# First cross attention of a Perceiver stack: score tiles of 32 by 32, two units a step in one PSUM tile, probabilities transposed on VectorE, one division a batch

## The chip, the cores and the metric

The kernel runs on one core of a Trainium2 chip. The metric is device time in microseconds (us), from one launch that holds the whole network. Three runs of the kernel before gave 3168.56, 3169.97 and 3195.57 us; the median is 3169.97 us.

## The reference, cut to what matters

The network has four layers of cross attention, self mixing (attention or a state space block) and feed-forward. Only the first block of the first layer is touched. It reads 16 batches of 64 query tokens with 256 channels and, per batch, 1024 context tokens with 192 channels.

```python
def _L0_xattn_ref(q_tokens, kv_tokens, Wq, Wk, Wv, Wo):   # (16,64,256), (16,1024,192)
    q = q_tokens @ Wq.T; k = kv_tokens @ Wk.T; v = kv_tokens @ Wv.T
    # 16 heads of 16 channels: (16, 16, 64 or 1024, 16)
    attn = einsum('bhqd,bhkd->bhqk', q, k) / sqrt(16)
    attn = softmax(attn, axis=-1)
    out = einsum('bhqk,bhkd->bhqd', attn, v)
    return merge_heads(out) @ Wo.T
x = x + _L0_xattn_ref(layernorm(x), ctx_768, Wq, Wk, Wv, Wo)
```

Everything is float32. A matmul of float32 stands in the trace as two records of load and two of multiply, so 4 matmuls appear as x8.

## The kernel before

The function is `xattn_direct`. Its loop runs over 64 **steps**, one for each batch `b` (16) and group of four heads `c` (4). Four heads of 16 channels fill 64 partitions. Each step works on three things at once: the scores of the next step (`ahead`), the probabilities of this one, and the values of the last one. Beside these it projects a quarter of the keys or values of the next batch (`project(b + 1, c)`).

The order on TensorE, VectorE and ScalarE is written out by hand: `mm`, `tr`, and the queues `dve` and `act` chain every instruction to the one before it on its engine (`in_order`), so an engine takes its instructions in exactly the order in which the Python code emits them. GpSimd (POOL) and the DMA queue SP follow the order that a scheduler gave them. Waits between engines are set by the tile framework from the tiles that two instructions touch.

One step before does this:

- `scores`: four matmuls of 32 rows by 128 columns over 512 keys each, into two PSUM tiles `pss` of two banks each (tag `s`). One tile holds two heads by 64 queries on its 128 partitions and 1024 keys.
- `least`: VectorE takes the negated maximum of each row, one reduction of 128x1024 for each tile.
- `exps`: ScalarE computes the exponential of a whole tile in one instruction (128x1024), with the row sum in `accum_out`.
- `shares`: VectorE inverts the sum and multiplies the 128x1024 probabilities with it.
- `transposes`: TensorE transposes 16 blocks of 128x128 against the identity into PSUM (`pst`), and VectorE and ScalarE copy them to `pT`, two copies each of 128x512.
- `values`: 32 matmuls of 128 rows by 32 columns into `both`, accumulated over the eight blocks of keys.
- `project`: eight matmuls, then one copy on VectorE and one on ScalarE.
- `keep` copies the finished output of a batch once in four steps, and `output` multiplies it with `Wo` once in eight.

PSUM has eight banks: four for the two `pss` tiles, three for the pool `ps_t` (`psp`, `pst`, `psq`, `psy`), one for `both`.

Of the kernel before, what the change touches and what calls it, by code (L numbers as in the profile page):

```python
# [15 lines left out]
P = 128  # L16
# [39 lines left out]
def bc(ap, axis, n):  # L56

    ap = ap.unsqueeze(axis)
    shape = list(ap.shape)
    shape[axis] = n  # L60
    return ap.to_broadcast(shape)
# [17 lines left out]
class Net:  # L79
# [200 lines left out]
    def xattn_direct(self, L):  # L280
# [5 lines left out]

        nc, tc, a = self.nc, self.tc, self.a
        dve, act = self.queue("dve", nc.vector), self.queue("act", nc.scalar)  # L290
        H = 16
# [4 lines left out]
        with ExitStack() as es:  # L296
            one = es.enter_context(tc.tile_pool(name=f"{L}one", bufs=1))
            two = es.enter_context(tc.tile_pool(name=f"{L}two", bufs=2))
            thr = es.enter_context(tc.tile_pool(name=f"{L}thr", bufs=2))
            ps_s = es.enter_context(tc.tile_pool(name=f"{L}ps_s", bufs=2, space=PSUM))  # L300
            ps_t = es.enter_context(tc.tile_pool(name=f"{L}ps_t", bufs=3, space=PSUM))
            ps_o = es.enter_context(tc.tile_pool(name=f"{L}ps_o", bufs=1, space=PSUM))

# [2 lines left out]
                own, self.ident.rearrange("p (g h d) -> p h g d", h=2, d=16), AX.XY, ALU.add  # L306
            )
            nc.vector.tensor_scalar(own, own, 0.25, None, ALU.mult)
            vs = [one.tile([P, NKC, H, 32], F32, name=f"v{i}") for i in range(2)]
            nc.gpsimd.memset(vs[0][:, :, :, 16:], 0.0)  # L310

# [38 lines left out]
                dve.tensor_scalar(qb[:, c, bs, 0, :], src, own[:, 0:1], None, ALU.mult)  # L350
                act.mul(qb[:, c, bs, 1, :], src, own[:, 1:2])

            ctxs, kTs, os_ = {}, {}, {}
            both = ps_o.tile([P, 2, 4, TQ], F32, name="o")

            def project(b, piece):

                if piece == 0:
                    ctxs[b] = self.load_ctxT(two, b)
                    kTs[b] = two.tile([P, 4, 512], F32, tag="kT", name="kT")  # L360
                c0, c1 = ctxs[b]
                ps = [ps_t.tile([P, 512], F32, tag="t", name="psp") for _ in range(2)]
                if piece < 2:

                    for i in range(2):
                        ms = slice((2 * piece + i) * 64, (2 * piece + i) * 64 + 64)
                        for n in range(2):
                            u = (n ^ i) * 64
                            self.mm(ps[i][u : u + 64, :], wk[:, 0, ms], c0[:, n * 512 : (n + 1) * 512], True, False)
                    for i in range(2):  # L370
                        ms = slice((2 * piece + i) * 64, (2 * piece + i) * 64 + 64)
                        for n in range(2):
                            u, rows = (n ^ i) * 64, slice(n * 64, (n + 1) * 64)
                            self.mm(ps[i][u : u + 64, :], wk[rows, 1, ms], c1[rows, :], False, True)
                    for i, copy in enumerate((dve.tensor_copy, act.copy)):
                        copy(kTs[b][:, 2 * piece + i, :], ps[i])
                else:
                    jh = piece - 2
                    v = vs[b % 2]

                    for n in range(2):
                        for i in range(2):
                            j = 4 * n + 2 * jh + i
                            self.mm(ps[n][:, i * D : (i + 1) * D], c0[:, j * P : (j + 1) * P], wv[:, 0, :], i == 0, False)
                    for i in range(2):
                        for n in range(2):
                            rows, jj = slice(n * 64, (n + 1) * 64), 2 * jh + i
                            self.mm(
                                ps[n][:, i * D : (i + 1) * D],
                                c1[rows, jj * P : (jj + 1) * P],  # L390
                                wv[rows, 1, :],
                                False,
                                i == 1,
                            )
                    for n, copy in enumerate((dve.tensor_copy, act.copy)):
                        j = 4 * n + 2 * jh
                        copy(v[:, j : j + 2, :, :16], ps[n].rearrange("p (i h d) -> p i h d", i=2, d=16))

            def scores(b, c):
                pss = [ps_s.tile([P, S], F32, tag="s", name="pss") for _ in range(2)]  # L400
                for n in range(2):
                    for e in range(2):
                        r = (n ^ (c % 2)) * 64 + e * 32
                        ql = qb[r : r + 32, c, b].rearrange("p h q -> p (h q)")
                        self.mm(pss[e][:, n * 512 : (n + 1) * 512], ql, kTs[b][r : r + 32, c, :])
                return pss

            def least(ps):
                nm = self.small.tile([P, 1], F32, tag="nm", name="nm", bufs=4)
                dve.tensor_reduce(nm, ps, AX.X, ALU.max, negate=True)  # L410
                return nm

            def exps(ps, nm):
                pr = thr.tile([P, S], F32, tag="pr", name="pr", bufs=4)
                sm = self.small.tile([P, 1], F32, tag="sm", name="sm", bufs=4)
                act.activation(pr, ps, AF.Exp, bias=nm, accum_out=sm)
                return pr, sm

            def shares(pr, sm):
                dve.reciprocal(sm, sm)  # L420
                dve.tensor_scalar(pr, pr, sm, None, ALU.mult)

            def transposes(dst, pr, jh, copy):
                pt = ps_t.tile([P, 512], F32, tag="t", name="pst")
                for j in range(4):
                    jj = jh * 4 + j
                    self.tr(pt[:, j * P : (j + 1) * P], pr[:, jj * P : (jj + 1) * P])
                copy(dst[:, jh * 4 : jh * 4 + 4, :], pt.rearrange("p (j q) -> p j q", q=P))

            def values(b, c, pT):  # L430
                o = both[:, b % 2]
                for j in range(NKC):
                    for h in range(4):
                        self.mm(
                            o[32 * h : 32 * h + 32, c, :],
                            vs[b % 2][:, j, 4 * c + h, :],
                            pT[:, j, h // 2, (h % 2) * TQ : (h % 2 + 1) * TQ],
                            j == 0,
                            j == NKC - 1,
                        )  # L440

            def keep(b):
                if b % 2 == 0:
                    os_[b // 2] = two.tile([P, 4, 2, TQ], F32, tag="oT", name="oT")
                act.copy(os_[b // 2][:, :, b % 2, :], both[:, b % 2])

            def output(t):
                ps = ps_t.tile([P, 512], F32, tag="t", name="psy")
# [8 lines left out]
            ins = nc.gpsimd.memset(vs[1][:, :, :, 16:], 0.0)  # L457
            tc.add_manual_dep(ins.ins, self.last_root.ins.name, order, reason="after the norm")
            normed(0)
            project(0, 0)  # L460
            project(0, 1)
            for c in range(4):
                queries(0, c)
            steps = [(b, c) for b in range(B) for c in range(4)]
            pss = scores(0, 0)
            prs = [exps(pss[e], least(pss[e])) for e in range(2)]
            project(0, 2)
            project(0, 3)
            for p in prs:
                shares(*p)  # L470
            last = None
            for i, (b, c) in enumerate(steps):
                ahead = steps[i + 1] if i + 1 < len(steps) else None
                nxt, nms = [None, None], [None, None]
                if ahead:
                    pss = scores(*ahead)
                    nms = [least(ps) for ps in pss]
                pT = thr.tile([P, NKC, 2, P], F32, tag="pT", name="pT")
                transposes(pT[:, :, 0, :], prs[0][0], 0, act.copy)
                transposes(pT[:, :, 0, :], prs[0][0], 1, dve.tensor_copy)  # L480
                if ahead:
                    nxt = [exps(pss[e], nms[e]) for e in range(2)]
                    shares(*nxt[0])
                if b + 1 < B:
                    project(b + 1, c)
                if last:
                    values(*last)
                if ahead:
                    shares(*nxt[1])
                transposes(pT[:, :, 1, :], prs[1][0], 0, dve.tensor_copy)  # L490
                transposes(pT[:, :, 1, :], prs[1][0], 1, act.copy)
                if i == 1:
                    norm(1)
                if i == 2:
                    normed(1)
                if 4 <= i < 8:
                    queries(1, i - 4)
                if c == 0 and last:
                    keep(b - 1)
                if c == 1 and b % 2 == 0 and b > 0:  # L500
                    output(b // 2 - 1)
                prs, last = nxt, (b, c, pT)
            values(*last)
            keep(B - 1)
            output(NT - 1)
            self.set_order(False)

# [2170 lines left out]
```

## Time and profile before

| What | us |
|---|---|
| median of three runs | 3169.97 |
| the profiled execution, its own time | 3170.8 |
| its span, first to last instruction | 3168.8 |
| first to last scores of this block | 462.3 (30.90 to 493.20) |
| TensorE busy in that stretch | 456.57 |
| VectorE busy in that stretch | 388.02 |
| ScalarE busy in that stretch | 261.59 |
| GpSimd busy in that stretch | 10.35 |

The profile is of one execution. Its page gives busy time by engine and by group of instructions; the trace behind it can be asked for the chain of work that ended last, for a timeline of a stretch, and for busy times in a stretch. TensorE stands in it twice, as PE (multiply) and PEld (load of weights), and a busy PE need not be at its peak, because multiplies overlap. All rows of this block carry line 72 (the queue helper), 188 (`mm`) or 191 (`tr`), so they are told apart by the names of their tiles. Rows called "copy", "reduce" and so on give the mean duration of one instruction.

### The profile page before, as it was taken

Reading aid. Unit: us, or ns where it says so; the run is one execution under the profiler, and the core shown is the slowest. Engines: PE = TensorE matmul, PEld = TensorE weight load, DVE = VectorE, ACT = ScalarE, POOL = GpSimd, SP = SyncE. Lnnn points to the kernel's source line nnn. Section 1 sums busy time; section 2 is a strip of 40 time slices with the busy share of each in tenths; the row PEclk is TensorE's granted clock in tenths of the full one; section 3 lists DMA queues with packets and bytes.
Section 4 is the critical chain, followed back from the end, with each engine's and each line's share of the span. In section 5 each row is a group of like instructions: output and inputs, shape, how many; then the busy total and the mean of one; then the engine's idle time right before and its main releaser. Section 6 shows DMA issues by size and latency. Waiting matters only on the chain.

```text
span 3168.8 us, 64106 instructions
## 1 busy us (share of the span) xinstructions
PE 2940.9 (93%) x26912; PEld 1772.9 (56%) x26912; DVE 1960.3 (62%) x4061; ACT 1348.4 (43%) x3035; POOL 712.7 (22%) x784
## 2 busy tenths in 40 slices
PE   7999999898899999979978999997999899998797
PEld 4666666665445544458854545434665455556676
DVE  6888886524666665971127676757884676765611
ACT  3555554312554541013324454438861255654211
POOL 1000002411110001014411000024771355541131
PEclk9999999999999999978988999998999999999889
DMA  2000000013223313017851222201111211210233
GB/s 74 32 32 32 28 22 15 14 37 105 61 78 92 98 45 82 21 65 270 294 162 53 70 71 73 59 21 39 41 54 37 64 57 63 70 44 14 94 108 122
DMA packets 73793, 223.00 MB, mean 70 GB/s; under 512 B 17457, under 2 KB 28580, under 8 KB 66594
## 3 DMA queue, kind: packets, MB, share of 16 engines
q1 hardware_dynamic: 45936, 113.99, 11.9%
q0 software_dynamic: 21840, 99.39, 9.4%
q10 hardware_dynamic: 5730, 5.53, 0.6%
q8 instruction: 212, 3.47, 0.5%
q14 instruction: 75, 0.61, 0.1%
HBM read 210.00 MB, written 12.66 MB: 70 GB/s over the span
## 4 chain that ended last, share of the span: by engine, by line
PE 79%; DVE 9%; issue 4%; ACT 4%; POOL 3%; DMA 1%; SPq 0%; ACTq 0%; POOLq 0%; DVEq 0%
PE pss L188 13%; PE o L188 12%; PE pu L188 6%; PE psp L188 5%; PE pkv L188 5%; PE pd L188 5%; PE py L188 4%; PE pst L191 4%; PE psc L188 3%; PE po L188 2%; DVE nm L72 2%; ACT pr L72 2%; PE pb L191 2%; PE psi L188 1%; PE psq L188 1%
## 5 line engine op out<-in xcount | busy, mean ns | idle before, releaser
L188 PE MATMUL pss<-cT,qw 128*32 128x256 f32 x8192 | 371.5, 387 | 23.0 <-ACT pr L72 23.0
L72 DVE TENSOR_REDUCE nm<-pss 128x2 f32<-128x512 f32 (+1 forms) x384 | 309.3, 861 | 86.3 <-PE pss L188 86.3
L188 PE MATMUL o<-pT,cx 128*64 128x512 f32 (+1 forms) x1024 | 355.4, 607 | 0.0
L72 ACT ACTIVATE pr<-pss,nmm 128x256 f32<-128x256 f32 x512 | 234.3, 483 | 164.8 <-DVE nmm L72 164.8
L188 PEld LDWEIGHTS pss<-cT,qw 128*32 128x32 f32 x8192 | 205.0, 110 | 173.0 <-ACT pr L72 33.1
L188 PEld LDWEIGHTS o<-pT,cx 128*64 128x64 f32 (+1 forms) x1024 | 127.8, 165 | 200.2 <-issue 187.8
L205 POOL TENSOR_SCALAR rs<-mv 128x8 f32<-128x8 f32 (+3 forms) x52 | 10.0, 193 | 877.1 <-DVE mv L221 444.4
L188 PE MATMUL pkv<-wx,cT 128*128 128x512 f32 (+1 forms) x512 | 193.3, 632 | 0.6 <-issue 0.6
L72 ACT ACTIVATE pr<-pr,sm 128x256 f32<-128x256 f32 x256 | 109.1, 497 | 184.2 <-DVE sm L72 184.2
L72 DVE TENSOR_SCALAR pr<-pr,sm 128x256 f32<-128x256 f32 (+1 forms) x384 | 170.6, 486 | 6.6
L72 DVE TENSOR_TENSOR_SCAN h<-dA,pb 128x512 f32<-128x512 f32 x128 | 154.5, 1217 | 15.8 <-PE pb L191 9.4
L1444 POOL TENSOR_TENSOR h<-h,cb 128x1024 f32<-128x1024 f32 x64 | 151.4, 2368 | 53.3 <-DVE h L72 51.0
L2304 DVE TENSOR_SCALAR y<-pd,row 128x256 f32<-128x256 f32 x39 | 18.9, 484 | 225.1 <-PE pd L188 175.7
L72 DVE STREAM_TRANSPOSE pT<-pr 128x1024 f32<-128x1024 f32 x128 | 151.8, 1224 | 2.2
L188 PE MATMUL pd<-wd,hT 128*128 128x256 f32 x656 | 149.3, 382 | 3.0 <-DVE hT L2492 1.4
L72 ACT ACTIVATE pr<-pss,nm 128x1024 f32<-128x1024 f32 x128 | 142.5, 1113 | 11.4 <-DVE nm L72 8.8
L191 PE MATMUL pst<-ident,pr 128*128 128x128 f32 x1024 | 140.6, 280 | 5.8 <-DVE sm L72 1.9
L72 ACT COPY pT<-pst 128x512 f32<-128x512 f32 x128 | 74.9, 585 | 163.8 <-PE pst L191 163.8
L191 PEld LDWEIGHTS pst<-ident,pr 128*128 128x128 f32 x1024 | 109.4, 141 | 61.5 <-ACT pT L72 26.5
L188 PEld LDWEIGHTS pd<-wd,hT 128*128 128x128 f32 x656 | 123.1, 190 | 31.4 <-DVE hT L2492 6.2
L1618 POOL TENSOR_TENSOR rnk<-rnk,mhalf 128x8 f32<-128x8 f32 (+1 forms) x84 | 130.0, 1548 | 7.0
L188 PE MATMUL py<-h,ident 128*128 128x512 f32 x256 | 130.7, 596 | 0.0
(525 smaller groups left out, 5700.2 us busy)
## 6 DMA issues: line engine op xcount, KB each, us to landing
cT<-in_ctxT SPq DMA_DIRECT2D x32, 768.0 KB, 4.4
cx<-in_ctxP SPq DMA_DIRECT2D x32, 768.0 KB, 4.3
cT<-in_ctxT SPq DMA_DIRECT2D x32, 512.0 KB, 4.3
cT<-in_ctxT SPq DMA_DIRECT2D x64, 256.0 KB, 6.1
offb<-d_off SPq DMA_DIRECT2D x16, 576.0 KB, 3.6
cb<-d_C SPq DMA_DIRECT2D x16, 512.0 KB, 3.8
wu<-in_L_ffn_w POOLq DMA_DIRECT2D x8, 1024.0 KB
wd<-in_L_ffn_w POOLq DMA_DIRECT2D x8, 1024.0 KB
```

Source lines behind the costliest of these rows:

```text
L72: ins = getattr(self.engine, op)(*args, **kwargs)
L188: self.in_order(self.nc.tensor.matmul(out, lhsT=lhsT, rhs=rhs, start=start, stop=stop))
L191: self.in_order(self.nc.tensor.transpose(out, in_, self.ident))
L205: nc.gpsimd.tensor_scalar(t[:p, :n], in_, scale, eps, ALU.mult, ALU.add)
L1444: nc.gpsimd.tensor_tensor(hs[i], hs[i], cbs[hf, g], ALU.mult)
L1618: nc.gpsimd.tensor_tensor(r, r, self.mhalf[:, : n * H], ALU.pow)
L2304: nc.vector.tensor_scalar(y[:, i, :], po[:, i * D : (i + 1) * D], weight[:, g + i : g + i + 1], None, ALU.mult)
```

## The change

The change rewrites the middle of the step. The scores of one step are now split into two halves `hh`, each with two of the four heads, 64 queries and all 1024 keys. Keys are dealt to partitions by quarters: the matmuls are 32 rows by 32 columns and fill 16 tiles of the array, so that partition 32 qa + x holds query x against the keys of quarter qa. There is now one PSUM tile `pss` for both halves, allocated once, and in each of its four banks the two halves stand beside each other.

The maximum of a query now lies on four partitions: `largest` reduces on VectorE, GpSimd moves the four quarters beside each other (`nw`), `least` reduces again, and GpSimd copies the result back to all partitions (`nmm`). `exps` is four instructions for each half. `turn` transposes the probabilities in blocks of 32 by 32 on VectorE, straight from SBUF to `pT`; the transposes on TensorE, the multiplication by 1/sum and the copies out of `pst` are gone. Outputs are divided once a batch: `sums` adds the sums of the four quarters on TensorE, VectorE inverts them, GpSimd spreads them out (`rd`), `spread` brings them to the layout of the output, ScalarE copies (`ra`) and `keep` multiplies on VectorE. Both copies after `project` are now on ScalarE.

```diff
-            ps_s = es.enter_context(tc.tile_pool(name=f"{L}ps_s", bufs=2, space=PSUM))
+            ps_s = es.enter_context(tc.tile_pool(name=f"{L}ps_s", bufs=1, space=PSUM))
...
+            pss = ps_s.tile([P, 2, 4, 2, P], F32, name="pss")
...
-            def scores(b, c):
-                pss = [ps_s.tile([P, S], F32, tag="s", name="pss") for _ in range(2)]
-                for n in range(2):
-                    for e in range(2):
-                        r = (n ^ (c % 2)) * 64 + e * 32
-                        ql = qb[r : r + 32, c, b].rearrange("p h q -> p (h q)")
-                        self.mm(pss[e][:, n * 512 : (n + 1) * 512], ql, kTs[b][r : r + 32, c, :])
+            def scores(b, c, hh):
+                kT = kTs[b][:, c].rearrange("p (k a y) -> p k a y", a=4, y=32)
+                for u in range(2):
+                    for qa in range(4):
+                        for n in range(2):
+                            for e in range(2):
+                                r = (n ^ (c % 2)) * 64 + e * 32
+                                self.mm(
+                                    pss[qa * 32 : (qa + 1) * 32, n, 2 * e + u, hh, :],
+                                    qb[r : r + 32, c, b, hh, u * 32 : (u + 1) * 32],
+                                    kT[r : r + 32, :, qa, :],
+                                )
+            def largest(hh):
+                nm = self.small.tile([P, 4], F32, tag="nm", name="nm", bufs=4)
+                dve.tensor_reduce(nm, pss[:, :, :, hh, :].rearrange("p n q k -> p q n k"), AX.XY, ALU.max, negate=True)
+                w = self.small.tile([32, 4, 4], F32, tag="nw", name="nw", bufs=4)
+                for qa in range(4):
+                    nc.gpsimd.tensor_copy(w[:, qa], nm[qa * 32 : (qa + 1) * 32])
+                return w
+            def least(w):
+                m = self.small.tile([P, 4], F32, tag="nmm", name="nmm", bufs=4)
+                dve.tensor_reduce(m[:32], w.rearrange("p a q -> p q a"), AX.X, ALU.min)
+                nc.gpsimd.tensor_copy(m[32:64], m[:32])
+                nc.gpsimd.tensor_copy(m[64:], m[:64])
+                return m
+            def exps(b, c, hh, m):
...
+                for q in range(4):
+                    act.activation(pr[:, q], pss[:, :, q, hh, :], AF.Exp, bias=m[:, q : q + 1],
+                                   accum_out=sms[b][:, c, hh, q : q + 1])
...
-            def transposes(dst, pr, jh, copy):
-                pt = ps_t.tile([P, 512], F32, tag="t", name="pst")
-                for j in range(4):
-                    jj = jh * 4 + j
-                    self.tr(pt[:, j * P : (j + 1) * P], pr[:, jj * P : (jj + 1) * P])
-                copy(dst[:, jh * 4 : jh * 4 + 4, :], pt.rearrange("p (j q) -> p j q", q=P))
+            def turn(b, c, hh, pr, lo=0, hi=4):
...
+                dve.transpose(
+                    pTs[b, c][:, :, hh, lo:hi].rearrange("p k q x -> p q k x"),
+                    pr[:, lo:hi].rearrange("p q n (k y) -> p q (n k) y", y=32),
+                )
...
+            def sums(b):
+                ps = both[:, 1].rearrange("p c q -> p (c q)")[:, :32]
+                for qa in range(4):
+                    self.mm(ps[qa * 32 : (qa + 1) * 32], same, sms[b].rearrange("p c h q -> p (c h q)"))
+                dve.reciprocal(rc, ps)
+                nc.gpsimd.tensor_tensor(rds[b]..., bc(rc, 2, 32), bc(same, 1, 32), ALU.mult)
+            def spread(b):
+                for h in range(4):
+                    self.mm(both[32 * h : 32 * h + 32, 1], fourth, rds[b][:, :, h % 2, h // 2, :])
+                act.copy(ra, both[:, 1])
...
             for i, (b, c) in enumerate(steps):
...
                 if ahead:
-                    pss = scores(*ahead)
-                    nms = [least(ps) for ps in pss]
-                transposes(pT[:, :, 0, :], prs[0][0], 0, act.copy)
-                transposes(pT[:, :, 0, :], prs[0][0], 1, dve.tensor_copy)
+                    scores(*ahead, 0)
+                    w = largest(0)
+                turn(b, c, 1, prs[1])
                 if ahead:
-                    nxt = [exps(pss[e], nms[e]) for e in range(2)]
-                    shares(*nxt[0])
+                    prs[0] = exps(*ahead, 0, least(w))
                 if b + 1 < B:
-                    project(b + 1, c)
+                    late = project(b + 1, c)
+                    act.copy(*late[0])
+                if ahead:
+                    scores(*ahead, 1)
+                    w = largest(1)
+                if c == 3:
+                    sums(b)
+                if c == 0 and last:
+                    ra = spread(b - 1)
                 if last:
                     values(*last)
                 if ahead:
-                    shares(*nxt[1])
-                transposes(pT[:, :, 1, :], prs[1][0], 0, dve.tensor_copy)
-                transposes(pT[:, :, 1, :], prs[1][0], 1, act.copy)
+                    turn(*ahead, 0, prs[0], 0, 2)
+                    prs[1] = exps(*ahead, 1, least(w))
+                    turn(*ahead, 0, prs[0], 2, 4)
+                if c == 0 and last:
+                    keep(b - 1, ra)
+                if b + 1 < B:
+                    act.copy(*late[1])
...
```

## The prediction

> **What bounds it now.** I began with the page's chain that ended last (PE holds 79% of it), then asked for the busy times of the stretch in which this block runs, from its first to its last scores, and then for the timeline of one step.
>
> ```profile
> span 3168.8 us, 64106 instructions
> PE 79%; DVE 9%; issue 4%; ACT 4%; POOL 3%; DMA 1%; SPq 0%; ACTq 0%; POOLq 0%; DVEq 0%
> 30.90:493.20 462.30, 456.57 (x6491) 283.87 (x6489) 388.02 (x605) 261.59 (x457) 10.35 (x13) 1.00 0.09 30
> ```
>
> The third line is the stretch: length, then busy PE, PEld, DVE, ACT, POOL, granted clock, DMA share. TensorE is busy 99% of it at full clock. The chain of waits inside it names TensorE alone, step after step:
>
> ```profile
> 205.43 1.09 PE L191 MATMUL pst<-ident,pr 128*128 128x128 f32 x8
> 206.46 1.14 PE L188 MATMUL pss<-kT,qb 32*128 32x512 f32 x8
> 207.53 1.09 PE L191 MATMUL pst<-ident,pr 128*128 128x128 f32 x8
> 208.46 2.96 PE L188 MATMUL psp<-wv,cT 128*128 128x256 f32 x16
> 211.34 1.10 PE L188 MATMUL o<-pT,v 128*32 128x64 f32 x64
> ```
>
> Each row starts as the one above ends: scores, transposes, projection, values, transposes, 6.94 to 7.03 us a step. Steps with `output` take 8.8; the mean is 462.3/63 = 7.34 us. The other engines hide because the step is a pipeline two tiles deep: VectorE reduces one `pss` tile while ScalarE exponentiates the other (reductions from 200.61 to 202.97, first exponential from 201.87).
>
> **The change, part by part.**
>
> *TensorE.* Transposes go: 2 x 1.03 = 2.06 us a step. The scores become 2 x 64 records of 128 columns. No row has 32x32 tiles; the nearest is this one:
>
> ```profile
> 905.90 1.96 PE L188 MATMUL pss<-cT,qw 64*32 64x256 f32 x64
> ```
>
> Eight tiles run at once there: 8 rounds of 0.216 us for 256 columns, the tail of one record 0.38, starts 7 ns apart. With 16 tiles and 128 columns a half is 4 rounds: 3 x 0.109 (the start distance of the 128-column transposes) + a tail of 0.27 + 16 x 0.007 = 0.72 us. If only four tiles ran at once it would be 16 rounds, 2.0 us. I take 0.72, since eight and four tiles both pack fully in the trace. TensorE's sum is then 2 x 0.72 + 2.9 + 1.1, 5.4 us a step.
>
> *VectorE.* Gone: two pairs of reciprocal and multiplication (0.15 + 0.75), two `pT` copies (0.68), one copy after `project` (0.69), 3.85 us. Added: 2.45 us of 32x32 transposes, from this row of a later block, and two small reductions of about 0.17 (the small `nw` rows take 0.16). From 6.2 us the sum falls to about 5.2.
>
> ```profile
> L72 DVE STREAM_TRANSPOSE pT<-pr 128x1024 f32<-128x1024 f32 x128 | 151.8, 1224 | 2.2
> ```
>
> *ScalarE.* Eight exponentials of 128x256 instead of two of 128x1024. A later block shows such a series:
>
> ```profile
> 787.44 0.46 ACT L72 ACTIVATE pr<-pss,nmm 128x256 f32<-128x256 f32 x1
> 787.80 0.20 ACT L72 ACTIVATION_READ_ACCUMULATOR pr<-pss,nmm 128x1 f32 x1
> 787.89 0.47 ACT L72 ACTIVATE pr<-pss,nmm 128x256 f32<-128x256 f32 x1
> ```
>
> One starts every 0.45 us; four with the last read of the sum take 3 x 0.45 + 0.59 = 1.94 us. With two copies of 0.59, about 5.1 a step.
>
> *GpSimd.* Twelve copies of a few bytes per step. No such row exists; the nearest are 0.19 for a 128x4 multiply-add and 0.23 for a 64x64 copy, and the smallest of any kind is a memset at 0.09. I take 0.18, and 0.57 for four in a row. Once a batch `rd` (128x1024, two inputs) comes in front of the last two copies in GpSimd's queue; the same shape takes this:
>
> ```profile
> L1444 POOL TENSOR_TENSOR h<-h,cb 128x1024 f32<-128x1024 f32 x64 | 151.4, 2368 | 53.3 <-DVE h L72 51.0
> ```
>
> No engine has more than 5.4 us of work a step. So the question is what waits for what.
>
> **The waits.** In the program of the changed kernel the first matmul of `scores(ahead, 1)` waits for the last exponential of half 0, and `largest(1)` waits for it too; the first matmul of `scores(ahead, 0)` waits for the last exponential of half 1. The two halves read and write different addresses, but they lie in the same four banks of the one `pss` tile.
>
> Here a rule of the Trainium skill speaks against the change. "PSUM — Partial Sum Buffer", section "PSUM bank collisions raise a hardware error", says that two engines may not be in one bank and partition quadrant at once, reads included, and that PSUM must be guarded by bank and quadrant and not by address. The row of before (reduction beside exponential) has the two in different banks, and so says nothing against it. By the row, overlap goes on; by the rule, scores, maxima and exponentials of the two halves take turns. The waits in the program follow the rule, and I take it.
>
> So one step is a single chain, twice from scores to exponentials. Hops by the trace: 0.05 after PE or ACT, 0.10 between DVE and POOL and into ACT, 0.08 from POOL to POOL.
>
> Half 0: hop 0.05, scores 0.72, hop 0.05, `largest` 1.22 (a 128x1024 reduction), `turn` of the half before 1.24 (it stands ahead of `least` in VectorE's queue and covers the four copies), `least` 0.17, hop 0.10, two copies 0.44, hop 0.10, exponentials 1.94: **6.03**.
>
> Half 1: the same, but between `largest` and `least` only half a `turn` (0.65) or hop, four copies and hop (0.72): **5.51**.
>
> Together 11.54 us for a step without extras. The projection (2.9) fits into the 5.3 us between the two scores on TensorE, values (1.1) and `output` (1.7) after the second; the late copies fit into ScalarE's waits. At no cost, thus; without that cover the projection alone would be 2.9 a step.
>
> Extras per batch: at c = 3 `rd` starts 0.67 after `largest`, takes 2.37, and the copies behind it start 2.1 us later than else. At c = 0 `values` waits for `spread` (0.62) and the copy `ra` (0.38), and `turn` waits for `values`: 0.95. Over 15 batches: 46 us.
>
> Stretch: 63 x 11.54 + 46 = 773 against 462: **+311**. Single costs: the first two halves one after the other +3; the last `rd` and `spread` +2; scaling `wo` for the next block (4 x 1.13 us, with a DMA of 4 us ahead) stands in GpSimd's queue before the copies of one half, +5.
>
> *Clock.* TensorE will now pause 3.6 us before half 0 (longer at c = 3) and 2.3 before half 1. "TensorE: Matmul & The Clock Gate", Part 1, says half rate comes after a whole idle window of about 3.4 us; by it a pause of 3.6 would almost never do it, and the cost is near zero. The trace is harsher: after a pause of 3.0 us a window at half clock follows.
>
> ```profile
> 788.05 0.16 PEld L188 LDWEIGHTS pss<-cT,qw 128*32 128x32 f32 x8 [3.48 <-ACT pr L72]
> 788.20:791.60 3.40, 3.40 (x36) 1.75 (x33) 2.26 (x2) 2.53 (x12) 0.00 (x0) 0.50 0.48 96
> ```
>
> By the row, about one of three steps has its first scores at half clock, 0.5 us each: +10. Half clock throughout would lengthen two scores, and values before `turn`: about 1.9 a step, +120.
>
> Sum: 311 + 3 + 2 + 5 + 10 = +331 on the profiled execution's own 3170.8 us (span 3168.8), which lies 1 us above the median of the runs. **Forecast 3502 us.**
>
> **Rivals.**
>
> *A, the halves overlap (faster).* If the waits within the banks were not there or never came last, the place would be VectorE and ScalarE alone: from the end of half 1's exponentials 1.24 `turn`, 0.17, 0.10, 0.44, 0.10, exponentials 1.94, late copy 0.59, exponentials 1.94 = 6.5 us a step, 63 x 6.5 = 410. With the 10 us of single costs 3170.8 - 52 + 10 = 3129. For it: every engine has room. Against it: the waits stand in the program. It decides as soon as a step lasts under 7.34 us.
>
> *B, TensorE is slower than its rows (slower still).* Either the 16 tiles don't run together, 2.0 instead of 0.72 for each half (+161), or the clock stays halved (+120): 3622 to 3663. For it: no row shows 32x32 tiles, and TensorE would be busy less than half of a step. Against it: 64x32 tiles pack fully, and before the trace got full clock back after one window.
>
> *C, the small steps on GpSimd are cheap.* At 0.09 a copy each half loses 0.18: 63 x 0.36 = 23 us, 3479. At 0.30 it is some 40 us dearer. Both are within the forecast's own range.
>
> **How the numbers follow.** Forecast with C's spread, hops uncertain by 0.3 us a half (38 us): 82%, 3440 to 3580. B 13%, A 3%, something between A and the forecast 2%. The range 3420 to 3625 takes in part of B. A measurement of this kernel can tell about 1% (32 us) from no change; A is just beyond that. Faster 0.03, same 0.01, slower 0.96.
>
> **What would show it.** Right: the chain of waits through the block runs in turn through `pss`, `nm`, `pT`, `nmm` and `pr`, TensorE is busy under half of the stretch, the steps are 11 to 13 us apart, and `pss` matmuls wait for `pr` twice a step. Each term can be read off: 0.72 from the first to the last `pss` record of a half, 1.94 from the first `pr` to the last, 0.44 for the pair of `nmm` copies, 2.4 for `rd`. Wrong: steps of 7 us or less, or matmuls of half 1 running beside exponentials of half 0.

## The result, and the profile after

The changed kernel takes **3572.64 us** (median of 5 runs, 3552.36 to 3575.49) against 3174.39 for the kernel before beside it (5 runs, 3168.56 to 3195.57). The ratio is **1.1219**, with a 95% interval of 1.1173 to 1.1265: slower, as forecast. It is 71 us above the forecast of 3502 and inside the range. The profiled execution took 3552.36 us, 381.6 more than that of before (3170.8).

First the span, then the row of the stretch from the first to the last scores of this block (length, then busy PE, PEld, DVE, ACT, POOL with their counts, granted clock, DMA share):

```profile
span 3550.7 us, 79980 instructions
28.04:872.75 844.71, 531.32 (x13362) 307.53 (x13360) 345.49 (x520) 313.57 (x1159) 173.64 (x790) 0.79 0.06 17
```

The stretch grew from 462.30 to 844.71, by 382.4 us: it holds the whole loss. TensorE went from 99% busy to 63%, at a mean clock of 0.79 instead of 1.00, and no other engine is busy for half of the time. Nothing is full; everything waits. The list of waits between 100 and 850 us (who waited for whom; us in total, times, longest) goes round in a ring; before, the chain of waits named TensorE alone:

```profile
POOL nw L434 <- DVE nm L72: 513.9, 112, 4.9
ACT pr L72 <- POOL nmm L442: 433.7, 110, 9.4
PEld pss L188 <- ACT pr L72: 296.6, 113, 7.5
PE pss L188 <- ACT pr L72: 244.7, 105, 7.2
DVE nm L72 <- PE pss L188: 233.9, 68, 5.3
```

The timeline of one half (start, length, engine, operation, and in brackets the idle time before it and its releaser) has it link by link; the second scores row is where the next half begins:

```profile
411.21 1.52 PE L188 MATMUL pss<-kT,qb 32*32 32x128 f32 x64 [3.96 <-ACT pr L72]
412.67 4.52 PE L188 MATMUL psp<-cT,wk 128*64 128x512 f32 x16
412.85 1.23 DVE L72 TENSOR_REDUCE nm<-pss 128x4 f32<-128x1024 f32 x1 [4.15 <-PE pss L188]
413.99 1.24 DVE L72 STREAM_TRANSPOSE pT<-pr 128x1024 f32<-128x1024 f32 x1
414.13 0.83 POOL L434 COPY nw<-nm 32x4 f32<-32x4 f32 x4 [4.94 <-DVE nm L72]
415.15 0.12 DVE L72 TENSOR_REDUCE nmm<-nw 32x4 f32<-32x16 f32 x1
415.40 0.18 POOL L441 COPY nmm<-nmm 32x4 f32<-32x4 f32 x1 [0.44 <-DVE nmm L72]
415.64 0.18 POOL L442 COPY nmm<-nmm 64x4 f32<-64x4 f32 x1
415.86 0.47 ACT L72 ACTIVATE pr<-pss,nmm 128x256 f32<-128x256 f32 x1 [4.22 <-POOL nmm L442]
417.84 1.07 PE L188 MATMUL pss<-kT,qb 32*32 32x128 f32 x64 [0.66 <-ACT pr L72]
```

From 411.21 to 417.84 each row starts as the one before it in the ring ends. Only the projection (412.67) and the four copies (414.13) run beside this: the copies are done at 414.96, but `least` (415.15) stands behind the turn (413.99) in VectorE's queue. Note that the same 64 scores take 1.52 us in the first row and 1.07 in the last: the first come after a pause of 3.96 us and run at half clock. The rows of these two stretches show it (the granted clock is the third number from the end):

```profile
411.21:412.73 1.52, 1.52 (x66) 1.02 (x67) 0.00 (x0) 0.42 (x1) 0.00 (x0) 0.50 0.00 0
417.84:418.90 1.06, 1.06 (x68) 0.77 (x72) 0.00 (x0) 0.42 (x1) 0.00 (x0) 1.00 0.00 0
```

For the experiments one measure is read from every trace: the time of a pass of the loop, from the maximum of its half 0 to that of the next pass, as a mean for each c. Each row is one profiled execution, and two executions of one kernel differ by up to some 30 us in all (0.5 us a pass).

| kernel | c=0 | c=1 | c=2 | c=3 |
|---|---|---|---|---|
| before | 7.00 | 8.18 | 7.11 | 7.06 |
| changed | 13.37 | 12.57 | 12.58 | 14.68 |
| no division | 12.63 | 12.63 | 12.56 | 12.89 |
| division moved | 12.54 | 12.62 | 12.61 | 14.76 |
| two tiles | 10.09 | 7.54 | 8.49 | 9.05 |
| two tiles, late turns | 8.82 | 7.34 | 8.32 | 9.41 |
| and rd behind | 7.63 | 7.10 | 8.39 | 9.14 |

### The profile page after: what moved, and what is told of

It reads as the page before. It is cut to its first block, busy times and chain, and to the rows that moved or that the text cites. A ratio compares the mean times of both kernels' runs of the same rounds, so it can differ in the third digit from the quotient of the medians.

```text
span 3550.7 us, 79980 instructions
## 1 busy us (share of the span) xinstructions
PE 3014.0 (85%) x33824; PEld 1796.0 (51%) x33824; DVE 1913.3 (54%) x3970; ACT 1396.2 (39%) x3735; POOL 879.2 (25%) x1568
## 4 chain that ended last, share of the span: by engine, by line
PE 58%; DVE 7%; issue 4%; ACT 4%; POOL 2%; DMA 1%; ACTq 0%; POOLq 0%; SPq 0%; DVEq 0%
PE pss L188 10%; PE o L188 9%; PE pu L188 5%; PE pd L188 5%; PE pkv L188 5%; PE py L188 4%; PE psc L188 3%; PE po L188 2%; ACT pr L72 2%; PE pb L191 2%; DVE nm L72 1%; PE psi L188 1%; PE pg L188 1%; PE psqw L188 1%; PE psy L188 1%
## 5 line engine op out<-in xcount | busy, mean ns | idle before, releaser
L72 ACT ACTIVATE pr<-pss,nmm 128x256 f32<-128x256 f32 x1024 | 469.7, 477 | 674.3 <-POOL nmm L442 494.5
L188 PE MATMUL pss<-kT,qb 32*32 32x128 f32 (+2 forms) x8576 | 199.1, 341 | 278.4 <-ACT pr L72 278.1
L72 DVE STREAM_TRANSPOSE pT<-pr 128x1024 f32<-128x1024 f32 (+1 forms) x319 | 319.2, 1018 | 42.5 <-PE o L188 38.4
L188 PEld LDWEIGHTS pss<-kT,qb 32*32 32x32 f32 (+1 forms) x8576 | 113.1, 116 | 365.3 <-ACT pr L72 335.0
L434 POOL COPY nw<-nm 32x4 f32<-32x4 f32 x512 | 90.6, 177 | 613.8 <-DVE nm L72 598.2
L72 ACT ACTIVATION_READ_ACCUMULATOR pr<-pss,nmm 128x1 f32 x1024 | 214.2, 209 | 0.0
L188 PE MATMUL psp<-wv,cT 64*128 64x256 f32 (+1 forms) x512 | 139.6, 502 | 3.8 <-DVE v L72 3.8
L188 PE MATMUL psp<-cT,wk 64*64 64x512 f32 (+1 forms) x512 | 138.5, 810 | 0.0
```

What stands on the lines that cost most here:

```text
L72: ins = getattr(self.engine, op)(*args, **kwargs)
L188: self.in_order(self.nc.tensor.matmul(out, lhsT=lhsT, rhs=rhs, start=start, stop=stop))
L434: nc.gpsimd.tensor_copy(w[:, qa], nm[qa * 32 : (qa + 1) * 32])
```

## The experiments

The theory to be tested: the halves take turns because they wait for each other within one `pss` tile; that is nearly the whole loss. The main rivals: the small copies on GpSimd, the slower scores, the clock.

### Own banks, one tile; then two tiles

The first kernel gives each half two PSUM banks of its own, but leaves one tile. The second makes two tiles of it; the matmuls are the same, but the two banks of a half now lie side by side, where before they were banks 0 and 2, or 1 and 3, of the one tile.

```
own banks:  pss = ps_s.tile([P, 2, 2, 4, P], F32, name="pss")     # half = pair of row strips
            pss[qa*32:(qa+1)*32, n, e, 2*h2 + u, :]               # bank 2*n + e
two tiles:  pss = [ps_s.tile([P, 2, 4, P], F32, ...) for i in range(2)]
            pss[hh][qa*32:(qa+1)*32, n, 2*h2 + u, :]
```

> The units are divided into the two halves by pair of row strips instead of by tile of heads, so that each half lies in two PSUM banks of its own; there is still one pss tile, and in the program the first scores of a half and its maximum still wait for the last exponential of the other half. Theory (the halves take turns because of the waits, and these follow the tile): nothing gained, 3573 within 40 us; the scores run on 8 tiles instead of 16, which at one weight load per 17 ns costs nothing. Rival (the shared banks themselves make engines wait, whatever the waits in the program): the step shortens from 13.4 us towards 7, and the time is under 3350. Second rival (8 tiles are slower than 16): 0.3 us more a half, about 3610.

Measured: 3587.8 us, ratio 1.1302 (1.1275 to 1.1328). Nothing gained. The granted clock was lower still, 0.76 in the stretch; at full clock the scores took 1.15 us on 8 tiles of the array against 1.07 on 16. The halves still wait for each other in every pass:

```profile
425.19 0.48 ACT L72 ACTIVATE pr<-pss,nmm 128x256 f32<-128x256 f32 x1
425.81 1.96 PE L188 MATMUL pss<-kT,qb 32*32 32x128 f32 x64 [3.42 <-ACT pr L72]
```

These are scores of half 0, and the first of them writes bank 0 of the tile. The exponential that they wait for reads banks 1 and 3. Neither a shared bank nor a range of addresses that covers both explains this wait; what the two share is the tile.

> As the kernel with own banks, but the two halves are two pss tiles; the program no longer has a wait between scores and maximum of one half and the exponentials of the other. Theory (taking turns is the whole loss): VectorE and ScalarE alone make the step. From the end of half 1's exponentials: turn 1.24, least and hops 0.3, copies 0.42, exponentials 1.84; then half a turn 0.65, least and hops 0.3, copies 0.42, exponentials 1.84: 7.0 us a step, 441, and 45 for the division, against 462 before: about 3195 us, 3160 to 3240. Rival (the small copies on GpSimd and scores at half clock make the loss): 3450 or more.

Measured: 3265.1 us, ratio **1.0282** (1.0253 to 1.031). One tile made into two takes 323 us off the kernel with own banks. In its timeline the maximum of one half runs while ScalarE still exponentiates the other. That is so for 106 of 126 maxima, and for none in the changed kernel and with own banks:

```profile
405.69 1.15 PE L188 MATMUL pss<-kT,qb 32*32 32x128 f32 x64
...
406.17 0.47 ACT L72 ACTIVATE pr<-pss,nmm 128x256 f32<-128x256 f32 x1 [1.43 <-POOL nmm L443]
...
406.90 1.23 DVE L72 TENSOR_REDUCE nm<-pss 128x4 f32<-128x1024 f32 x1 [1.31 <-PE pss L188]
...
407.08 0.47 ACT L72 ACTIVATE pr<-pss,nmm 128x256 f32<-128x256 f32 x1
```

So the wait that goes with the tile is the cause of about three quarters of the loss: of the 398 us 308 are gone. Separate banks were not enough. Two tiles in the *same* banks were not tried, nor two adjacent banks for each half in one tile.

The theory asked for nearly the whole loss, and the expected 3195 was missed by 70 us. The step of 7.0 us is near the passes with c = 1 (7.54). By the trace the others are longer through the division (c = 3 and 0) and through `output` in TensorE's queue (c = 2, every second batch); how much each costs here no run shows.

### Late turns, and what was tried to come below before

Two tiles, and each `turn` half a step later, so that `least` doesn't stand behind the turn of what has just been exponentiated:

```
-  turn(b, c, 1, prs[1])             +  turn(b, c, 0, prs[0])
   prs[0] = exps(*ahead, 0, least(w))
   ...
-  turn(*ahead, 0, prs[0], 0, 2)     +  turn(b, c, 1, prs[1])
   prs[1] = exps(*ahead, 1, least(w))
-  turn(*ahead, 0, prs[0], 2, 4)
```

> Two pss tiles as in the kernel with two tiles, and every turn comes half a step later, so that least is not behind the turn of the exponentials that ended last. Theory: the chain exponentials, turn, least, copies, exponentials is cut; what is left is the sum of the busiest engine, TensorE with 2 x 1.07 + 2.9 + 1.1 + 0.4 = 6.5 us a step, or VectorE with 5.2 and its waits: 6.5 to 7.0 us a step, 3130 to 3170 us. Rival (the turn in front of least only covers the four copies, and these set the time): no shorter than with two tiles alone, about 3195.

Measured: 3241.14 us, ratio 1.0202 (1.0173 to 1.023). A small gain, well short of the theory; the sum counted busy times only. One tile still needs scores, maximum, turn, least, copies and exponentials (1.15, 1.22, 1.24, 0.13, 0.6, 1.84, about 6.2 us) before it is free, and its scores stand in TensorE's queue behind up to 3 us of projection.

With the six copies on VectorE and `least` ahead of the turn:

```
-  nc.gpsimd.tensor_copy(w[:, qa], nm[...])   +  dve.tensor_copy(w[:, qa], nm[...])
   (and both copies in least);  m = least(w) before turn(...)
```

> Two pss tiles, every turn half a step later, the small copies of the maxima on VectorE, and least in front of the turn. In the run with two tiles and late turns a half took 4.28 us, and from the end of the maximum to the first exponential lay 2.0 us (the turn of 1.24, least, and the GpSimd copies with their hops). Theory (that latency, and not any engine's work, is what was left): it falls to about 0.8 us, a step is then bounded by TensorE's 6.5 to 7.2 us: 3115 to 3165 us, at or under before. Rival (the order scores, maximum, exponentials, scores of one tile with the projection in TensorE's queue sets the step): 3200 to 3241.

Measured: 3274.96 us, ratio 1.0315 (1.0297 to 1.0333), slower than with the copies on GpSimd. The theory was wrong about the price. The chain of the piece from 410 to 432 us, summed by line, and the copies in the timeline:

```profile
by line: DVE nm L72 31.8%; DVE pT L72 26.6%; DVE nw L72 15.5%; issue 12.2%; DVE nmm L72 11.0%; DVE st L220 2.0%; DVE X L72 1.4%; DVE oT L72 1.4%; DVE mv L221 0.2%; DVEq L72 0.1%
416.06 0.67 DVE L72 COPY nw<-nm 32x4 f32<-32x4 f32 x4
416.97 0.36 DVE L72 COPY nmm<-nmm 32x4 f32<-32x4 f32 x2
```

Sixteen bytes to a partition cost 0.17 us on VectorE as well, and there 1.03 us of copies (0.67 + 0.36) are added to a queue that already holds 1.22 and 1.24 in each half: in this piece VectorE is nearly the whole chain. Part of the 34 us lost against late turns probably lies elsewhere: in 14 of the 16 batches the pair of `nmm` copies ran beside `rd` and took some 2.04 us (last section).

The projection issued in two parts, one after each scores, and the division meant to be out of the way:

```
-  late = project(b + 1, c); act.copy(*late[0])   +  part = project(b + 1, c); act.copy(*part(0))
   ... scores(*ahead, 1) ...
-  act.copy(*late[1])                             +  act.copy(*part(1))
```

> Two pss tiles and late turns, and besides: the projection is issued in two parts, one after each scores; rd stands behind the second half's copies in GpSimd's queue; spread comes after values. With two tiles and late turns a half took 4.28 us; the scores of half 1 stood behind the whole projection in TensorE's queue, and the division cost some 3 us a batch. Theory (what is left after the waits is queueing, behind the projection and behind rd): 3.6 us a half, 7.2 a step, near before's 7.34: 3165 us, 3130 to 3190. Rival (the chain within one tile, from scores over maximum, turn, copies and exponentials to the next scores, sets the step whatever stands in the queues): 3210 to 3241.

Measured: 3265.61 us, ratio 1.0313 (1.0248 to 1.0377): a miss. It isn't a clean test either: the scheduler set `rd` ahead of the copies all the same, and the parts of the V projection no longer use both row halves of TensorE at once. A part took 2.19 us where the whole had taken 3.06. Splitting it in this way wins nothing; whether a split without that cost would, is open.

Last, late turns with `rd` held behind the copies by an ordering edge, and `spread` after `values`:

> Two pss tiles and late turns, whole projection; rd is now really behind the copies of half 1 in GpSimd's queue (in the two runs that only issued it later in the text the scheduler had set it in front of them again), and spread comes after values. In the run with two tiles and late turns a step after c = 1 took 7.3 us, after c = 2 (output) 8.3, after c = 3 9.4 and after c = 0 8.8; before took 7.34 in the mean. Theory (the extra of c = 3 and c = 0 is these two queue positions): both fall to about 7.4, the mean to 7.6, the time to some 3190 us, 3175 to 3210, no better than before. Rival (the chain within a tile takes the place of these waits): little is gained, 3220 or more.

Measured: 3238.43 us, ratio 1.0163 (1.0132 to 1.0195), which can't be told from late turns alone (3241.14). In the profile c = 0 fell from 8.82 to 7.63, as expected of `spread`, but the profiled execution of late turns was 23 us slower than its median, so part of the fall is that; c = 3 hardly moved (9.41 to 9.14). At c = 3 it is not `rd` that is late then, but this:

```profile
419.76 1.41 PE L188 MATMUL o<-pT,v 128*32 128x64 f32 x64 [1.48 <-DVE rc L72]
...
421.10 1.96 PE L188 MATMUL pss<-kT,qb 32*32 32x128 f32 x64
...
422.99 4.98 PE L188 MATMUL psp<-cT,wk 128*64 128x512 f32 x16
...
421.10:422.99 1.89, 1.89 (x68) 1.50 (x64) 0.00 (x0) 1.54 (x7) 1.75 (x3) 0.50 0.06 18
```

`values` waits for the reciprocal `rc`, since sums and outputs are in the one tile `both`; TensorE pauses, and the scores (1.96 instead of 1.15) and the projection (4.98 instead of 2.96) then run at half clock or little above (0.50 in the last row). No version beat the kernel before.

### Maxima on VectorE in the changed kernel

Only the six copies move from GpSimd to VectorE.

> The changed kernel with the six small copies of each half's maxima on VectorE instead of GpSimd; the halves still take turns. Theory (the copies and their hops are one link of the chain of each half, and once a batch rd stands in front of two of them): the pair after least goes from 0.13 + 0.42 to some 0.2, the four before it no longer overlap with the turn; 0.3 us a half less, -38, and rd no longer in the way at c = 3, some -1.5 us in each of 16 batches, -24: 3510 us, 3490 to 3535, still far above before. Rival 1 (GpSimd is the loss): under 3300. Rival 2 (VectorE is so full that the copies cost there what they save): 3560 to 3600.

Measured: 3625.59 us, ratio 1.1435 (1.1406 to 1.1464). Taking the copies from GpSimd does not bring the loss back; VectorE is worse, because its four copies now stand in front of the turn instead of running beside it. From the end of the maximum to the first exponential half 0 takes 2.53 us (401.54 to 404.07) instead of 1.78. The theory's gain of 38 was wrong: it took VectorE's small copies to be cheaper than 0.17 us.

### Scores twice

```
-  for u in range(2):
+  for u in (0, 1, 0, 1):
```

> Every matmul of scores is issued twice, into the same place (64 more in each of the 126 halves). Theory (the scores lie wholly on the chain, and TensorE is bound by one weight load per 17 ns): 64 x 17 ns = 1.07 us a half, +135, about 3705 us, up to 20 more where the clock is halved. Rival 1 (on the chain, but bound by the stream of 16 tiles, four rounds of 0.109): +55, about 3630. Rival 2 (off the chain, the small steps set the time): within 15 us of 3573.

Measured: 3703.97 us, ratio 1.168 (1.1646 to 1.1714): +131 us, so the scores lie wholly on the chain. The size came out right by luck: at full clock 64 more matmuls took 0.83 us (1.90 instead of 1.07), 13 ns each, not 17, which alone is 105 us over 126 halves; but nearly half of the scores ran at half clock, and there they took 1.30 us more (2.82 instead of 1.52). The mean of a half rose from 1.25 to 2.31 us, some 134 us in all.

### No division; division moved

```
no division:   sums, spread and ra left out;  keep: tensor_copy(os_, both[:, 0])
moved:         values(*last), then spread(b - 1);  rd in a function called after least(w)
```

> The changed kernel without the division: sums, the reciprocal, rd, spread and the copy ra are left out, and keep copies the undivided output. Theory (rd delays two copies once a batch, and spread with ra delays values): 46 us by the prediction's own sum, with rd at its measured 1.91 us instead of 2.37 some 40: 3530 us, 3515 to 3540. Rival (the division runs beside the chain): within 10 us of 3573.

Measured: 3514.14 us, ratio 1.1082 (1.1055 to 1.1109): 58 us less by the medians, 39 by the profiled spans (3550.7 to 3511.3; that of the changed kernel is the fastest of its five executions). The table shows where: without the division all passes take 12.6 to 12.9; with it c = 0 costs 0.7 more and c = 3 1.8, some 38 us over 15 batches.

> The changed kernel, its division complete, but rd is issued behind the copies of half 1 instead of in front of them, and spread with ra comes after values instead of before. Without any division the time was 3514, 58 us less than the changed kernel. Theory (these 58 us are two queue positions, not the work): most of it comes back, 3520 to 3535. Rival (the work itself costs wherever it stands): within 15 us of 3573.

Measured: 3546.28 us, ratio 1.1166 (1.1134 to 1.1197), an interval that overlaps that of the changed kernel. In the passes half of the expectation held: c = 0 fell from 13.37 to 12.54, so `spread` and `ra` cost only by their place. c = 3 stayed at 14.76, since the scheduler had set `rd` in front of the copies again; that part of the kernel did not do what it was meant to.

### The clock: values twice, and matmuls that nobody reads

> The changed kernel with values issued twice, the second time over the first with the same result: 1.1 us more of TensorE work in each step, in a time in which it would be idle, so that its pauses get shorter. Theory (some 37% of the scores run at half clock and take 1.52 instead of 1.07 us, 21 us in all, because of the pauses): part of that comes back, 3552 to 3570 us, granted clock up by 0.02 or more. Rival (the clock costs nothing, or the extra work falls on the chain): 3573 to 3640, the longer end if values hold up the turn or the next scores.

Measured: 3621.59 us, ratio 1.1422 (1.1398 to 1.1445). The rival's longer end: the second `values` holds up the turn, and the turn `least`.

```profile
410.12 0.71 DVE L72 STREAM_TRANSPOSE pT<-pr 128x512 f32<-128x512 f32 x1 [0.67 <-PE o L188]
```

So this kernel says nothing on the clock. It shows that `values` in half 1 has next to no slack. The next one adds work for which nothing waits:

```
def filler(c, rounds):    # c = 1 and 2: 4 rounds after the projection, 10 after values
    self.mm(both[32*h : 32*h + 32, 1, :2, :], fourth, self.ident)    # for h in range(4)
```

> The changed kernel with matmuls that nobody reads in two of every four steps (c = 1 and 2): 16 after the projection and 40 after values, some 0.5 and 1.2 us, in times in which TensorE was idle. Nothing waits for them. Theory (pauses of 3 us and more bring windows at half clock, and these cost 0.45 us for each scores that falls into one): in the filled steps the share of scores at half clock falls well under that of the others, and the time by 5 to 12 us. Rival (the windows come whatever TensorE does in between): the same share in all steps, and 3573 to 3590.

Measured: 3559.86 us, ratio 1.1224 (1.118 to 1.1268), which can't be told from the changed kernel's 1.1219. The records support the mechanism: TensorE's pause before the half-0 scores that follow a filled pass fell to about 1 us and to none (medians; 3.95 and 2.03 in the changed kernel), and none of these scores were at half clock, against 9 of 16 and 8 of 15; after the passes without filler it stayed at 13 of 16 and 14 of 15. Over all halves the scores' mean fell from 1.25 to 1.20 us, some 7 us in all. The time did not follow: the mean wait from the last exponential to the next scores grew from 0.17 to 0.24 us a half, some 9 us in all, because the filler, or `output` behind it, was sometimes still in TensorE's queue. What the clock costs as a whole is therefore only read off the records (below), not shown by a run.

## Why the prediction was right, and where its sizes were off

- **The waits: right.** The forecast was a ring through `pss`, `nm`, `pT`, `nmm` and `pr`, with TensorE far from full, and the list of waits shows it. Two tiles end it, and with it three quarters of the loss. The waits were read off the program. The reason given for them, "they lie in the same four banks", was wrong; by luck it leads to the same waits in this kernel. I had taken the waits to follow the rule of the Trainium skill, "PSUM — Partial Sum Buffer", section "PSUM bank collisions raise a hardware error", that PSUM is guarded by bank and quadrant. Own banks in one tile kept the waits and the time, so in this program they follow the tile. No run here shows what two engines in one bank would do.
- **The sum of a step: 11.54 forecast, 12.57 measured** (c = 1 and 2). The mis-sized term is the scores, **0.72** a half. They take 1.07 at full clock, 0.35 more in each of 126 halves: 44 us. The forecast took 16 tiles to run at once with one tile's starts 7 ns apart. The records of one half show the first 32 matmuls some 7 ns apart, then a step of 0.18 us, and most of the next 32 some 17 ns apart. On 8 tiles they take 1.15, so the second eight bring almost nothing. The truth lies between the forecast's 0.72 and rival B's 2.0. The ground for the lower end, that eight and four tiles pack fully in the trace of before, did not carry over to sixteen of a quarter of the size.
- **The clock: 10 forecast, about 22.** The row of before (half clock after a pause of 3.0 us) was nearer than the rule of the Trainium skill, "TensorE: Matmul & The Clock Gate", Part 1, of a whole idle window of some 3.4 us: of the half-0 scores after a pause of 3.4 us 15 of 16 had a mean granted clock under 0.75, and by the rule hardly any would; after 3.7 us and more it was 31 of 34, but after 2.0 to 2.1 us only 2 of 9. The mis-sized term is the share: 71% of the half-0 scores (44 of 62) took over 1.3 us, not a third; with 4 of half 1 that is 48 halves times 0.45 us. The projections at half clock (4.5 us instead of 2.9) cost next to nothing here; in the timeline the projection ends 0.66 us before the next scores start.
- **The other terms** nearly cancel. The exponentials with the last read of the sum came out (1.93 instead of 1.94), and so did the hop after them (0.05); the last hop into ScalarE took 0.03 instead of 0.10; `nm` to `least` in half 0 1.07 instead of 1.24 (the turn's record starts before that of the maximum ends); in half 1 0.93 instead of 0.72 (four copies on GpSimd take 0.83, not 0.57); the hop after the scores 0.11 instead of 0.05. Together they add under 0.1 us a step.
- **The division: 46 forecast; 39 to 58 by the run without it.** Passes at c = 0 cost 0.8 more than those at c = 1 and 2 (0.95 forecast), and at c = 3 2.1 (2.1 forecast). The second agrees in size but not in its working, which laid it all on `rd`:

```profile
406.15 1.10 PE L188 MATMUL o<-pT,v 128*32 128x64 f32 x64 [1.46 <-DVE rc L72]
406.80 1.91 POOL L486 TENSOR_TENSOR rd<-rc,same 128x1024 f32<-128x1024 f32 x1
407.32 0.71 DVE L72 STREAM_TRANSPOSE pT<-pr 128x512 f32<-128x512 f32 x1 [1.22 <-PE o L188]
407.96 0.12 DVE L72 TENSOR_REDUCE nmm<-nw 32x4 f32<-32x16 f32 x1
408.77 0.18 POOL L441 COPY nmm<-nmm 32x4 f32<-32x4 f32 x1
```

  `values` waits for `rc`, the turn for `values`, `least` for the turn: `least` starts at 407.96, 2.1 us after the maximum instead of 0.93. Only then is `rd` in the way, for some 0.6 us (`least` ends at 408.08, the copy comes at 408.77). And the scores after it come at half clock more often (14 of 15, against 17 of 31 after c = 1 and 2), some 0.2 us in the mean. With the copies on VectorE, where `rd` stands in no queue before them, passes at c = 3 still cost 2.2 us more (15.98 against 13.7).
- **What was to show it.** Passes of 11 to 13 us: yes at c = 1 and 2, 13.4 and 14.7 at c = 0 and 3. Scores that wait for `pr` in every half: yes, 113 such waits beside 112 of the first copy in the list. TensorE busy for under half of the stretch: no, 63%: the scores took 158 us of its time and not 91, the projections 271 and not 180, by the slower scores and the half clock. The pair of `nmm` copies 0.44: 0.42. `rd` 2.4: 1.91.
- **The sum of the misses**: scores +44, clock +12 and, by difference, the rest -6, is the 50 us between +331 forecast and +381.6 in the profiled execution. The other 20 us to the median of 3572.64 is what lies between that execution and the other runs.
- **Rival A, 3129 with overlap:** the overlap did not come in this kernel, and its price was wrong too. With two tiles, where the halves do overlap, the kernel takes 3265, and 3238 with the best of the further steps. The rival summed VectorE and ScalarE and left out TensorE's queue, the division, `output` and the clock.

## What to carry to other kernels

Before a tile is shared by two halves that are to overlap, ask which waits the program will hold: here they went by the tile, and two tiles of half the size were worth 323 us against one, where other banks were worth nothing. Taking work from the bounding engine makes a kernel faster only if the ring of waits that remains is shorter than the step was: 6.1 us of TensorE work a step (two scores of 1.07, 2.9 and 1.1) are no gain in a ring of 12.6 where the step took 7.34. A moved instruction is moved only if the program's order, and not the text, has it in the new place.

## What was not expected of the hardware

- 32x32 scores on 16 tiles (1.07 us for 64 matmuls) are hardly quicker than on 8 (1.15); another 64 cost 0.83. The weight loads of such a half have 0.80 us of records, which fits a bound by loads, but a limit of eight tiles at once fits too; the runs don't tell them apart.
- Copies of 16 bytes to a partition cost about 0.17 us on VectorE, and 0.18 on GpSimd. Beside `rd` on GpSimd VectorE's were far slower, 2.04 us for the pair instead of 0.36 (from the kernel with two tiles and the copies on VectorE):

```profile
397.72 1.91 POOL L487 TENSOR_TENSOR rd<-rc,same 128x1024 f32<-128x1024 f32 x1 [32.49 <-DVE rc L72]
397.81 2.04 DVE L72 COPY nmm<-nmm 32x4 f32<-32x4 f32 x2
```

  The pair ends only when `rd` has ended. This kernel has it in 14 of 16 batches, with 1.97 to 2.05 us each time, and in no pair that ran without `rd`. Other work of VectorE was not slowed: in the changed kernel half a turn beside `rd` took 0.71 us (407.32 above), as without it. Why, no run shows.
